# Softmax sums and reciprocals of two attention groups at a time, in a convolution layer with attention on one Trainium2 core

## The chip, the cores and the metric

The kernel runs on one core of one Trainium2 chip, in one launch, all data in 32-bit floats. The metric is device time in microseconds (us): the median of three runs before the change is 2254.44, from 2254.12 to 2254.50. Beside these runs one execution was recorded by the hardware profiler; durations of single instructions, waits and stretches come from that execution.

The engines are named as in the profile: PE is TensorE (PEld its weight loads), DVE is VectorE, ACT is ScalarE, POOL is GpSimd, and SP is SyncE, which issues most of the DMAs.

## The reference

The input is eight images of 512 channels, 32x32 pixels. The layer is `x + layer(groupnorm(x))`, where the layer is (cbs is a convolution, a batch norm with fixed statistics, and SiLU; C = 256, HEADS = 4, HD = 64, N = 2):

```python
def bot_attention(x, qkv_w, rw, rh):
    b, c, h, w = x.shape
    hw = h * w
    qkv = conv2d(x, qkv_w, 0).reshape(b, 3, HEADS, HD, hw)
    q, k, v = (qkv[:, 0], qkv[:, 1], qkv[:, 2])
    r = (rw + rh).reshape(1, HEADS, HD, hw)
    logits = jnp.einsum('bhdi,bhdj->bhij', q, k + r) * HD ** (-0.5)
    a = jax.nn.softmax(logits, axis=-1)
    out = jnp.einsum('bhij,bhdj->bhdi', a, v)
    return out.reshape(b, c, h, w)
t = cbs(x, cv1_w, cv1_bn, 0)
ys = [t[:, :C], t[:, C:]]
for i in range(N):
    yi = ys[-1]
    z = cbs(yi, m_cv1_w[i], m_cv1_bn[i], 1)
    z = bot_attention(z, m_qkv_w[i], m_rw[i], m_rh[i])
    z = jax.nn.silu(bn_eval(conv2d(z, m_cv2_w[i], 0), m_cv2_bn[i]))
    ys.append(yi + z)
return cbs(jnp.concatenate(ys, axis=1), cv2_w, cv2_bn, 0)
```

cv1, cv2 and m_cv2 are 1x1 convolutions, m_cv1 is a 3x3 one. The change concerns the softmax of the attention: the sum over the keys j for each query i, and the division by it.

## The kernel before

The eight images run as four pairs. In each pair every image passes cv1, and then twice the 3x3 convolution (over tiles of transformed inputs, L653 its matmuls), the projection to q, k and v (L886 to L1000), the attention and m_cv2 (m2, L1270). That makes 16 attentions. The long 1x1 products are built from sums of blocks, so that there are fewer matmuls. Work of other stages is threaded into an attention by hand: `behind` is a dictionary of hooks, keyed by the place in the attention, whose functions issue a step each of the next image's group norm (L718, L719, L725, L734 to L737), of the Winograd-like tile pieces (L559 to L608), of filters, or of the next product.

`attention_fast` works on four groups g = 0 to 3, each one chunk c of two heads and one half of the 1024 queries: (0,0), (0,1), (1,0), (1,1). A group has eight key blocks, taken in pairs, so that there are 16 pairs. Iteration i issues

- the logits of pair i (L1037, eight matmuls in the 64x64 form, which make 16 records of the profile), their exponentials on ScalarE (L1041), and the addition of the exponentials on VectorE into `acc` (L1055 for a group's first pair, which has no acc to add to, else L1057);
- then the product of pair i-1 with v (L1071), which adds up in `av_ps`.

At a group's end `av_ps` is copied out by ScalarE (L1078: one half) and VectorE (L1079: adds the other half to it, into z). `av_ps` comes from a PSUM pool with one buffer, so the next group's first L1071 waits for L1079 of this one. The pool of the logits has three buffers (tag "big"), which the sums (`s_ps`), m2 and the 1x1 products share. `acc` has two buffers in SBUF.

The sums over the partitions of a group's acc are made one group later, at the border: between the logits of the second pair of group g and the first product with v of group g, `sums(g - 1)` issues four matmuls of ones and acc (L1088, the 128x32 form, eight records). ScalarE copies the result to a row (L1094), and four DMAs on SP's queue and one reciprocal take it on its way: the row to DRAM (L1095), back in 128 partitions of eight numbers (`total`, L1124), the reciprocal (L1131), to DRAM again (L1133), and out to all partitions of a head (L1135, two DMAs of 128 KB for a group). The trip from L1124 on is issued in the third pair of group g (`spread`), and z is multiplied by it (`scale`, L1143) in the second pair of group g + 1.

The last group's sums, spread and scale are given to the caller, and stand in the next stage: group 2's scale follows directly on the last copy-out, and group 3's is issued after a part of the next product or projection. Then comes m2: for each half and each of two output chunks oc it adds k = 0 and k = 1. In the order of the code m2's eight matmuls need groups 0, 2, 0, 2 (first half) and 1, 3, 1, 3. The very first attention treats its last group by itself (`at_once`, L1105 and after).

The order on each engine comes from a scheduler that follows the order of the code, except where `issue_after` ties a step to another, and moves matmuls whose data are late behind others.

In the attentions 1, 5 and 9 the code threads tile pieces of the next convolution (from L555 on, each ends with a `yield`) at the keys (1, 3), (2, 1), (2, 3), 3 and (3, 2), where pairs and groups count from 0 and (g, n) stands after the products of pair n of group g with v; in attention 13 it does so at every (g, n) with n from 1 to 3. The piece at (1, 3) computes w_g (L566).

Of the kernel before, what the change touches and what calls it, by code (L numbers as in the profile page):

```python
# [44 lines left out]
F32 = mybir.dt.float32  # L45
# [7 lines left out]
P = 128  # L53
# [3 lines left out]
HD = 64  # L57
# [4 lines left out]
def kernel(  # L62
# [16 lines left out]
    nc = tc.nc  # L79
# [8 lines left out]
    HALF = 512  # L88
# [10 lines left out]
    NG = NM * NH  # L99
# [5 lines left out]
    act = fast.enter_context(tc.tile_pool(name="act", bufs=1))  # L105
# [167 lines left out]
    s_dram = [tc.dram_tile([P, KB, CO], F32, name=f"s{i}") for i in range(4)]  # L273
# [217 lines left out]
    def stages(act, small, ps_big, ps_av, n_pt):  # L491
# [522 lines left out]
        def attention_fast(qkv, ao, at, behind, at_once=False):  # L1014
# [35 lines left out]
            def add_up(pair):  # L1050
                g, j0 = pair[0]
                pt = pts[pair[0]]
                if j0 == 0:
                    accs[g] = act.tile([P, 2, HALF], F32, tag="acc", name="acc", bufs=2)
                    return nc.vector.tensor_tensor(accs[g], pt[0], pt[1], ALU.add)  # L1055
                for i in range(PAIR):
                    ins = nc.vector.tensor_tensor(accs[g], accs[g], pt[i], ALU.add)  # L1057
                return ins
# [19 lines left out]
                    nc.scalar.copy(dst, av[:, 0])  # L1078
                    evicted[0] = nc.vector.tensor_tensor(dst, av[:, 1], dst, ALU.add)  # L1079

            def sums(g):

                NQ4 = HALF // 2
                ps = ps_big.tile([P, NQ4], F32, tag="big", name="s_ps")
                acc = accs.pop(g)
                for at_q in range(4):
                    hd, part = divmod(at_q, 2)
                    nc.tensor.matmul(  # L1088
                        ps[at_q * 32 : (at_q + 1) * 32, :], ones[:, 0:32], acc[:, hd, ts(part, NQ4)],
                        start=True, stop=True, tile_position=(0, at_q * 32),  # L1090
                    )
                s_dram = tc.dram_tile([4, NQ4], F32, name=f"s_dram{at + g}")
                row = act.tile([P, NQ4], F32, tag="h", name="s_row", bufs=2)
                nc.scalar.copy(row, ps)  # L1094
                nc.sync.dma_start(s_dram, row[0:P:32, :])  # L1095
                return s_dram

            def last_sums(g):
# [20 lines left out]
                nc.sync.dma_start(cs, s_dram.rearrange("k h (i r) -> (h i) k r", r=QP))  # L1119
                nc.vector.tensor_tensor(sums_all[:, at + g, :], cs[:, 0], cs[:, 1], ALU.add)  # L1120

            def total(g, s_dram):

                nc.sync.dma_start(sums_all[:, at + g, :], s_dram.rearrange("a (i r) -> (a i) r", r=QP))  # L1124
                return sums_all[:, at + g, :]

            def spread(g, s_dram):

                rs = act.tile([P, HALF], F32, tag="rs", name="rs", bufs=4)
                rc = small.tile([P, QP], F32, tag="rc", name="rc", bufs=2)  # L1130
                inverted[0] = nc.vector.reciprocal(rc, total(g, s_dram))  # L1131
                r_dram = tc.dram_tile([2, HALF], F32, name=f"r_dram{at + g}")
                nc.sync.dma_start(r_dram.rearrange("h (i r) -> (h i) r", r=QP), rc)  # L1133
                for hd in range(2):
                    spread_out[0] = nc.sync.dma_start(  # L1135
                        rs[hd * HD : (hd + 1) * HD, :], r_dram[hd : hd + 1, :].to_broadcast([HD, HALF])
                    )
                return rs

            def scale(g, rs):  # L1140
                c, half = groups[g]
                dst = ao[:, c, ts(half, HALF)]
                return nc.vector.tensor_tensor(dst, dst, rs, ALU.mult)  # L1143

            NQ = NJ // PAIR
            s_drams, rss, evicted = {}, {}, [None]
            for i in range(len(pairs) + 1):
                if i < len(pairs):
                    added = logits(pairs[i])
                    g, at_q = divmod(i, NQ)  # L1150
                    with tc.issue_after(added.ins):
                        if at_q == NQ - 2 and g > 0:
                            rss[g - 1] = spread(g - 1, s_drams[g - 1])
                        if i == 1:
                            later()
                        if at_q == 1 and g > 1:
                            scale(g - 2, rss.pop(g - 2))
                if i > 0:
                    g, j0 = pairs[i - 1][0]
                    if j0 == 0 and g > 0:  # L1160
                        s_drams[g - 1] = sums(g - 1)
                    times_v(pairs[i - 1])
                    if i < len(pairs) and accs.get(pairs[i][0][0], 0) is None:
                        with tc.issue_after(evicted[0].ins):
                            added = add_up(pairs[i])
                    with tc.issue_after(added.ins):
                        behind.get(g if j0 == 0 else (g, j0 // PAIR), lambda: None)()
# [2 lines left out]

            g = len(groups) - 1
            if not at_once:
                with tc.issue_after(evicted[0].ins):
                    scale(g - 1, rss.pop(g - 1))
                return SimpleNamespace(
                    evicted=evicted[0], added=added,
                    sums=lambda: s_drams.update({g: sums(g)}),
                    spread=lambda: rss.update({g: spread(g, s_drams[g])}),
                    scale=lambda: scale(g, rss.pop(g)),
                )  # L1180
            ps, rows, s_dram = last_sums(g)
            with tc.issue_after(added.ins):
                behind.get(len(groups) + 1, lambda: None)()
            with tc.issue_after(evicted[0].ins):
                scale(g - 1, rss.pop(g - 1))
            rs = act.tile([P, HALF], F32, tag="rs", name="rs", bufs=4)
            nc.vector.tensor_tensor(rs, ps[:, 1, :], rows[0], ALU.add)
            nc.vector.reciprocal(rs, rs)
# [631 lines left out]
    for p in range(NP):  # L1820
# [117 lines left out]
        def hooks(norms, us={}, extra={}):  # L1938
            calls = {}
            for g in range(NG):  # L1940
                for at in range(4):
                    key = (g, at) if at else g
                    calls[key] = [step_norm] if key in norms else []
                    calls[key] += [step_u] * us.get(4 * g + at, 0)
                    if key in extra:
                        calls[key].append(extra[key])
            return {key: (lambda fs: lambda: [f() for f in fs])(fs) for key, fs in calls.items()}
# [126 lines left out]
            parts_at = (part for i in (1, 2) for part in tiles_later(i))  # L2074

        def step_part():
            next(parts_at, None)

        at_keys = ((1, 3), (2, 1), (2, 3), 3, (3, 2)) if more else [(g, at) if at else g for g in range(NG) for at in range(1, 4)]
        behind = hooks(NORM_B, {0: 1, 1: 1, 4: 1}, {key: step_part for key in at_keys})  # L2080
        if not more:
            tops = load_tops(ib, Y1[1])
            top_w = [take(("w2", j)) for j in range(2)]
            w2_top = lambda k: top_w[k // 2][:, k % 2]
            ys = {0: tops}

            def rhs_direct(k, half):
                part, c = divmod(k, NM)
                if part < 2:
                    return ys[0][half][part][:, c]  # L2090
                return ys[1][half][part - 2][:, c]
# [23 lines left out]
        def spread():  # L2115
            end.spread()
            return s.inverted[0]
# [246 lines left out]
```

## Time and profile before

| | us |
|---|---|
| median of three runs | 2254.44 |
| lowest, highest | 2254.12, 2254.50 |
| profiled execution: time | 2252.28 |
| profiled execution: span, first to last instruction | 2250.8 |
| TensorE busy in it | 2209.8 |
| VectorE, ScalarE, GpSimd busy | 1728.8, 1101.3, 225.1 |
| logits L1037 and products with v L1071, busy | 486.4, 485.9 |
| sums over partitions L1088: busy, records | 40.3, 504 |
| row copies L1094: busy, instructions | 23.9, 63 |
| reciprocals L1131: busy, instructions | 12.4, 63 |
| scales L1143: busy, instructions | 43.9, 64 |

The granted TensorE clock has a mean of 0.998 of full speed. Busy times count an instruction from its start to its end as the profile has it; records of TensorE overlap, so their sum is more than the time they cost. A line of groups names the line of the code, the engine, the operation, output and inputs by their names in the program, partitions by elements, how many there are, the busy time and the mean of one in ns, and after it the idle time of the engine before these instructions with what ended it. A line of the timeline has the start (us from the span's start), the time to the end of the last of its instructions, the engine, the line and the operation; in brackets, how long the engine stood idle before it and what ended that.

### The profile page before, as it was taken

What the parts mean: (1) busy time and instruction counts of PE and PEld (TensorE: products, weight loads), DVE (VectorE), ACT (ScalarE), POOL (GpSimd) and SP (SyncE); (2) the same over time, 40 slices, a digit from 0 to 9 for tenths busy, and PEclk for the clock granted to TensorE, in tenths of its full rate; (3) what the DMA queues carried; (4) which work ended last, traced back from release to release, by engine and by line L of the source; (5) the groups of instructions that cost most, each with busy time, mean ns of one, the idle gap of its engine ahead of it and who ended that gap; (6) DMA issues with size and microseconds to landing.
All of it is one profiled execution on the core that took longest, in us unless ns stands there. A gap on an engine that the chain in (4) does not pass through costs nothing.

```text
span 2250.8 us, 40563 instructions
## 1 busy us (share of the span) xinstructions
PE 2209.8 (98%) x16346; PEld 1079.1 (48%) x16346; DVE 1728.8 (77%) x2675; ACT 1101.3 (49%) x1359; POOL 225.1 (10%) x417
## 2 busy tenths in 40 slices
PE   7999999999999999999999999999999999999998
PEld 3653437343474445633447343654345733473443
DVE  7988879878678688877947868986794868796652
ACT  7554653644225765465324667355622455335533
POOL 4322210000220000000021000000012000000001
PEclk9999999999999999999999999999999999999999
DMA  9855447221581324521257151632136611351214
GB/s 276 309 157 150 155 148 260 91 93 50 135 269 59 113 88 143 178 64 65 66 154 260 30 173 35 198 111 82 51 79 176 226 44 34 102 192 35 67 46 111
DMA packets 135284, 285.63 MB, mean 127 GB/s; under 512 B 34512, under 2 KB 62156, under 8 KB 134064
## 3 DMA queue, kind: packets, MB, share of 16 engines
q1 hardware_dynamic: 103184, 197.34, 26.5%
q0 software_dynamic: 31904, 85.61, 13.2%
q8 instruction: 131, 2.15, 0.4%
q14 instruction: 65, 0.53, 0.1%
HBM read 214.86 MB, written 68.03 MB: 126 GB/s over the span
## 4 chain that ended last, share of the span: by engine, by line
PE 82%; DVE 11%; issue 3%; ACT 2%; DMA 1%; POOL 0%; SPq 0%; DVEq 0%; POOLq 0%; ACTq 0%
PE av_ps L1071 17%; PE l_ps L1037 16%; PE c L1290 9%; PE c_ps L653 7%; PE c_new L1290 6%; PE p_ps L916 6%; PE ps L523 5%; PE m_ps L1270 5%; PE x_ps L1390 4%; PE p_ps L922 3%; DVE acc L1057 1%; PE s_ps L1088 1%; PE p_ps L886 1%; DVE c_e L680 1%; ACT ypad L495 0%
## 5 line engine op out<-in xcount | busy, mean ns | idle before, releaser
L1041 ACT ACTIVATE pt<-l_ps 128x1024 f32<-128x1024 f32 x512 | 495.7, 1023 | 339.5 <-PE l_ps L1037 228.0
L1057 DVE TENSOR_TENSOR acc<-acc,pt 128x1024 f32<-128x1024 f32 x384 | 469.7, 1223 | 60.4 <-ACT pt L1041 34.9
L1037 PE MATMUL l_ps<-q,kr 64*64 64x512 f32 x4096 | 486.4, 590 | 2.4 <-ACT pt L1041 1.5
L1071 PE MATMUL av_ps<-pt,vT 64*64 64x512 f32 x4096 | 485.9, 591 | 1.8 <-DVE z L1079 1.5
L1037 PEld LDWEIGHTS l_ps<-q,kr 64*64 64x64 f32 x4096 | 158.0, 133 | 272.1 <-issue 251.0
L1071 PEld LDWEIGHTS av_ps<-pt,vT 64*64 64x64 f32 x4096 | 155.1, 133 | 275.3 <-issue 250.6
L653 PE MATMUL c_ps<-v_in,u 128*64 128x128 f32 x4320 | 239.1, 273 | 2.5 <-issue 2.5
L653 PEld LDWEIGHTS c_ps<-v_in,u 128*64 128x64 f32 x4320 | 235.8, 137 | 9.3 <-issue 9.3
L1270 PE MATMUL m_ps<-z,m_sb 128*128 128x512 f32 x256 | 112.5, 592 | 0.0
L658 ACT COPY c_m<-c_ps 128x512 f32<-128x512 f32 x48 | 28.1, 586 | 169.9 <-PE c_ps L653 153.1
L916 PE MATMUL p_ps<-t_z,sq 128*128 128x512 f32 x224 | 107.0, 595 | 0.0
L1079 DVE TENSOR_TENSOR z<-av_ps,z 128x512 f32<-128x512 f32 x64 | 44.0, 688 | 73.5 <-ACT z L1078 73.4
L495 ACT ACTIVATE t<-m_ps,bh,sh 128x512 f32<-128x512 f32 x64 | 46.3, 774 | 86.5 <-PE m_ps L1270 86.5
L916 PE MATMUL p_ps<-z,sq 128*128 128x512 f32 x168 | 80.1, 604 | 4.4 <-ACT z L495 4.3
L1055 DVE TENSOR_TENSOR acc<-pt 128x1024 f32<-128x1024 f32 x64 | 77.8, 1216 | 6.8 <-ACT pt L1041 6.8
L1340 POOL DMA_DIRECT2D c_out<-in_x_dram x56 | 50.3, 972 | 280.2 <-ACT c_out L495 276.8
L1270 PEld LDWEIGHTS m_ps<-z,m_sb 128*128 128x128 f32 x256 | 48.3, 190 | 58.8 <-issue 57.4
L1143 DVE TENSOR_TENSOR z<-z,rs 128x512 f32<-128x512 f32 x64 | 43.9, 686 | 26.0 <-DMA rs<-r_dram 25.9
L495 ACT ACTIVATE c_out<-cz,bh,sh 128x512 f32<-128x512 f32 x14 | 16.7, 1294 | 90.4 <-DVE cz L1367 90.4
L495 ACT ACTIVATE z<-z,bh,sh 128x512 f32<-128x512 f32 x64 | 47.7, 804 | 25.0 <-DVE z L704 24.3
L1390 PE MATMUL x_ps<-t_x,sw 128*128 128x512 f32 x128 | 55.9, 592 | 0.0
L922 PEld LDWEIGHTS p_ps<-sq,z 128*128 128x128 f32 x336 | 42.9, 191 | 26.3 <-issue 12.5
(313 smaller groups left out, 3153.7 us busy)
## 6 DMA issues: line engine op xcount, KB each, us to landing
u<-u SPq DMA_DIRECT2D x135, 512.0 KB
rs<-r_dram SPq DMA_DIRECT2D x126, 128.0 KB
sq<-sq SPq DMA_DIRECT2D x42, 384.0 KB
x<-in_x_dram SPq DMA_DIRECT2D x28, 512.0 KB
r_in<-r SPq DMA_DIRECT2D x28, 512.0 KB
y_in<-y SPq DMA_DIRECT2D x28, 512.0 KB
c_out<-in_x_dram POOLq DMA_DIRECT2D x56, 256.0 KB, 5.4
out_dram<-c_out POOLq DMA_DIRECT2D x56, 256.0 KB, 3.7
```

The costliest lines, as they stand in the source:

```text
L495: silued[0] = nc.scalar.activation(dst, src, AF.Silu, scale=sh[:, k : k + 1], bias=bh[:, k : k + 1])
L523: last_product[0] = nc.tensor.matmul(ps[:, half, :], w_of(k), rhs_of(k, half), start=(k == begin), stop=(k == end))
L653: conv_product[0] = nc.tensor.matmul(to[o], us[cp][:, k, row, c, o], rhs, start=(k == 0), stop=(k == NM - 1),)
L916: nc.tensor.matmul(ps[:, o, :], w[:, o, :], rhs, start=not onto, stop=True, skip_group_check=onto)
L922: nc.tensor.matmul(v[:, ts(j, P)], rhs[:, ts(j, P)], w[:, 2, :], start=j == 0 and not onto, stop=True, skip_group_check=True,)
L1037: nc.tensor.matmul(ps[kh * HD : (kh + 1) * HD, hd, :], kr[r, c, o : o + HD], q[r, c, ts(half, HALF)], start=True, stop=True,)
L1041: last_exp[0] = exp = nc.scalar.activation(pt, ps, AF.Exp, scale=SCALE)
L1057: ins = nc.vector.tensor_tensor(accs[g], accs[g], pt[i], ALU.add)
L1071: nc.tensor.matmul(avs[g][hd * HD : (hd + 1) * HD, kh, :], vT[r, j, o : o + HD], pt[i][r, hd, :], start=(j == 0), stop=(j == NJ - 1),)
L1270: nc.tensor.matmul(pss[half][:, oc, :], m2_sb[:, n, k, ts(oc, P)], ao[:, k, ts(half, HALF)], start=(k == 0), stop=(k == NM - 1),)
L1290: nc.tensor.matmul(ps[:, o, :], w[:, k, ts(o, P)], rhs[part][:, c], start=(k == 0 and not onto), stop=(k == KB - 1), skip_group_check=onto,)
L1390: nc.tensor.matmul(ps[:, o, :], w[:, c, ts(o, P)], rhs[c], start=(c == 0 and not onto), stop=(c == 1), skip_group_check=onto,)
```

## The change

The sums, the row copy, the DMA to DRAM and back, the reciprocal and the DMA of the reciprocals are made for two groups at a time, over one PSUM tile, one row and one DRAM tile: groups 0 and 1 at the border where group 2 begins, groups 2 and 3 after the end of the attention (attention 0, `at_once`: groups 0 and 1 together, group 2 by itself). The rs DMAs stay two for each group. The scales of groups 0 and 1 both stand in the second pair of group 3, and those of 2 and 3 both where group 3's stood. acc keeps its two buffers. A hook ("border", 2) is called at the border of group 2, between the copy-out and the group's first addition; in the attentions that carry tile pieces one piece moves there from the key (1, 3).

```diff
@@ -1078,21 +1078,22 @@
                     nc.scalar.copy(dst, av[:, 0])
                     evicted[0] = nc.vector.tensor_tensor(dst, av[:, 1], dst, ALU.add)
 
-            def sums(g):
+            def sums(gs):
 
                 NQ4 = HALF // 2
-                ps = ps_big.tile([P, NQ4], F32, tag="big", name="s_ps")
-                acc = accs.pop(g)
-                for at_q in range(4):
-                    hd, part = divmod(at_q, 2)
-                    nc.tensor.matmul(
-                        ps[at_q * 32 : (at_q + 1) * 32, :], ones[:, 0:32], acc[:, hd, ts(part, NQ4)],
-                        start=True, stop=True, tile_position=(0, at_q * 32),
-                    )
-                s_dram = tc.dram_tile([4, NQ4], F32, name=f"s_dram{at + g}")
-                row = act.tile([P, NQ4], F32, tag="h", name="s_row", bufs=2)
+                ps = ps_big.tile([P, len(gs), NQ4], F32, tag="big", name="s_ps")
+                for n, g in enumerate(gs):
+                    acc = accs.pop(g)
+                    for at_q in range(4):
+                        hd, part = divmod(at_q, 2)
+                        nc.tensor.matmul(
+                            ps[at_q * 32 : (at_q + 1) * 32, n, :], ones[:, 0:32], acc[:, hd, ts(part, NQ4)],
+                            start=True, stop=True, tile_position=(0, at_q * 32),
+                        )
+                s_dram = tc.dram_tile([len(gs), 4, NQ4], F32, name=f"s_dram{at + gs[0]}")
+                row = act.tile([P, len(gs), NQ4], F32, tag="h", name="s_row", bufs=2)
                 nc.scalar.copy(row, ps)
-                nc.sync.dma_start(s_dram, row[0:P:32, :])
+                nc.sync.dma_start(s_dram.rearrange("g a i -> a g i"), row[0:P:32])
                 return s_dram
 
             def last_sums(g):
@@ -1119,29 +1120,38 @@
                 nc.sync.dma_start(cs, s_dram.rearrange("k h (i r) -> (h i) k r", r=QP))
                 nc.vector.tensor_tensor(sums_all[:, at + g, :], cs[:, 0], cs[:, 1], ALU.add)
 
-            def total(g, s_dram):
-
-                nc.sync.dma_start(sums_all[:, at + g, :], s_dram.rearrange("a (i r) -> (a i) r", r=QP))
-                return sums_all[:, at + g, :]
-
-            def spread(g, s_dram):
-
-                rs = act.tile([P, HALF], F32, tag="rs", name="rs", bufs=4)
-                rc = small.tile([P, QP], F32, tag="rc", name="rc", bufs=2)
-                inverted[0] = nc.vector.reciprocal(rc, total(g, s_dram))
-                r_dram = tc.dram_tile([2, HALF], F32, name=f"r_dram{at + g}")
-                nc.sync.dma_start(r_dram.rearrange("h (i r) -> (h i) r", r=QP), rc)
-                for hd in range(2):
-                    spread_out[0] = nc.sync.dma_start(
-                        rs[hd * HD : (hd + 1) * HD, :], r_dram[hd : hd + 1, :].to_broadcast([HD, HALF])
-                    )
-                return rs
+            def total(gs, s_dram):
+                dst = sums_all[:, at + gs[0] : at + gs[0] + len(gs), :]
+                nc.sync.dma_start(dst, s_dram.rearrange("g a (i r) -> (a i) g r", r=QP))
+                return dst
+
+            def spread(gs, s_dram):
+
+                rc = small.tile([P, len(gs), QP], F32, tag="rc", name="rc", bufs=2)
+                inverted[0] = nc.vector.reciprocal(rc, total(gs, s_dram))
+                r_dram = tc.dram_tile([len(gs), 2, HALF], F32, name=f"r_dram{at + gs[0]}")
+                nc.sync.dma_start(r_dram.rearrange("g h (i r) -> (h i) g r", r=QP), rc)
+                rss = []
+                for n in range(len(gs)):
+                    rs = act.tile([P, HALF], F32, tag="rs", name="rs", bufs=4)
+                    for hd in range(2):
+                        spread_out[0] = nc.sync.dma_start(
+                            rs[hd * HD : (hd + 1) * HD, :], r_dram[n, hd : hd + 1, :].to_broadcast([HD, HALF])
+                        )
+                    rss.append(rs)
+                return rss
 
             def scale(g, rs):
                 c, half = groups[g]
                 dst = ao[:, c, ts(half, HALF)]
                 return nc.vector.tensor_tensor(dst, dst, rs, ALU.mult)
 
+            def scale_all(gs):
+                for g, rs in zip(gs, rss.pop(gs)):
+                    ins = scale(g, rs)
+                return ins
+
+            batch = {1: (0, 1), 2: (2,)} if at_once else {1: (0, 1), 3: (2, 3)}
             NQ = NJ // PAIR
             s_drams, rss, evicted = {}, {}, [None]
             for i in range(len(pairs) + 1):
@@ -1149,19 +1159,22 @@
                     added = logits(pairs[i])
                     g, at_q = divmod(i, NQ)
                     with tc.issue_after(added.ins):
-                        if at_q == NQ - 2 and g > 0:
-                            rss[g - 1] = spread(g - 1, s_drams[g - 1])
+                        if at_q == NQ - 2 and g - 1 in batch:
+                            gs = batch[g - 1]
+                            rss[gs] = spread(gs, s_drams[gs])
                         if i == 1:
                             later()
-                        if at_q == 1 and g > 1:
-                            scale(g - 2, rss.pop(g - 2))
+                        if at_q == 1 and g - 2 in batch:
+                            scale_all(batch[g - 2])
                 if i > 0:
                     g, j0 = pairs[i - 1][0]
-                    if j0 == 0 and g > 0:
-                        s_drams[g - 1] = sums(g - 1)
+                    if j0 == 0 and g - 1 in batch:
+                        s_drams[batch[g - 1]] = sums(batch[g - 1])
                     times_v(pairs[i - 1])
                     if i < len(pairs) and accs.get(pairs[i][0][0], 0) is None:
                         with tc.issue_after(evicted[0].ins):
+                            before = behind.get(("border", pairs[i][0][0]), lambda: None)() or evicted[0]
+                        with tc.issue_after(before.ins):
                             added = add_up(pairs[i])
                     with tc.issue_after(added.ins):
                         behind.get(g if j0 == 0 else (g, j0 // PAIR), lambda: None)()
@@ -1170,19 +1183,18 @@
 
             g = len(groups) - 1
             if not at_once:
-                with tc.issue_after(evicted[0].ins):
-                    scale(g - 1, rss.pop(g - 1))
+                gs = batch[g]
                 return SimpleNamespace(
                     evicted=evicted[0], added=added,
-                    sums=lambda: s_drams.update({g: sums(g)}),
-                    spread=lambda: rss.update({g: spread(g, s_drams[g])}),
-                    scale=lambda: scale(g, rss.pop(g)),
+                    sums=lambda: s_drams.update({gs: sums(gs)}),
+                    spread=lambda: rss.update({gs: spread(gs, s_drams[gs])}),
+                    scale=lambda: scale_all(gs),
                 )
             ps, rows, s_dram = last_sums(g)
             with tc.issue_after(added.ins):
                 behind.get(len(groups) + 1, lambda: None)()
             with tc.issue_after(evicted[0].ins):
-                scale(g - 1, rss.pop(g - 1))
+                scale_all(batch[g - 1])
             rs = act.tile([P, HALF], F32, tag="rs", name="rs", bufs=4)
             nc.vector.tensor_tensor(rs, ps[:, 1, :], rows[0], ALU.add)
             nc.vector.reciprocal(rs, rs)
@@ -2074,10 +2086,11 @@
             parts_at = (part for i in (1, 2) for part in tiles_later(i))
 
         def step_part():
-            next(parts_at, None)
-
-        at_keys = ((1, 3), (2, 1), (2, 3), 3, (3, 2)) if more else [(g, at) if at else g for g in range(NG) for at in range(1, 4)]
+            return next(parts_at, None)
+
+        at_keys = ((2, 1), (2, 3), 3, (3, 2)) if more else [(g, at) for g in range(NG) for at in range(1, 4) if (g, at) != (1, 3)]
         behind = hooks(NORM_B, {0: 1, 1: 1, 4: 1}, {key: step_part for key in at_keys})
+        behind["border", 2] = step_part
         if not more:
             tops = load_tops(ib, Y1[1])
             top_w = [take(("w2", j)) for j in range(2)]
```

## The prediction, on record before the run

> Attentions are counted 0 to 15 in the order they run, groups 0 to 3 inside each; a border is where one group ends and the next begins. Line numbers are those of the kernel before.
>
> **What bounds the kernel now.** I read the page first: which engine is full, and what the chain that ended last consists of.
>
> ```profile
> span 2250.8 us, 40563 instructions
> ...
> PE 2209.8 (98%) x16346; PEld 1079.1 (48%) x16346; DVE 1728.8 (77%) x2675; ACT 1101.3 (49%) x1359; POOL 225.1 (10%) x417
> ...
> PE 82%; DVE 11%; issue 3%; ACT 2%; DMA 1%; POOL 0%; SPq 0%; DVEq 0%; POOLq 0%; ACTq 0%
> ```
>
> TensorE is the bound, and only 41 us of the span are left in which it does nothing. So the change pays only in TensorE time, and whatever it delays elsewhere costs as soon as TensorE waits for it. Next the groups that the change touches:
>
> ```profile
> L1079 DVE TENSOR_TENSOR z<-av_ps,z 128x512 f32<-128x512 f32 x64 | 44.0, 688 | 73.5 <-ACT z L1078 73.4
> L1143 DVE TENSOR_TENSOR z<-z,rs 128x512 f32<-128x512 f32 x64 | 43.9, 686 | 26.0 <-DMA rs<-r_dram 25.9
> ...
> L1088 PE MATMUL s_ps<-acc,ones 128*32 128x256 f32 x504 | 40.3, 391 | 2.2 <-DVE gm L734 1.4 <-DVE acc L1057 0.6
> ```
>
> 504 records are 63 stretches of 8 (attention 0 has three, its last group goes another way). What one stretch costs is not 8 x 391 ns, since records overlap; it is read from the starts, in the timeline round an ordinary border:
>
> ```profile
> 703.62 1.90 PE L1037 MATMUL l_ps<-q,kr 64*64 64x512 f32 x16
> ...
> 705.34 1.90 PE L1071 MATMUL av_ps<-pt,vT 64*64 64x512 f32 x16
> ...
> 707.05 1.90 PE L1037 MATMUL l_ps<-q,kr 64*64 64x512 f32 x16
> ...
> 707.92 0.69 DVE L1079 TENSOR_TENSOR z<-av_ps,z 128x512 f32<-128x512 f32 x1
> ...
> 708.53 1.22 DVE L1055 TENSOR_TENSOR acc<-pt 128x1024 f32<-128x1024 f32 x1
> ...
> 708.88 0.64 PE L1088 MATMUL s_ps<-acc,ones 128*32 128x256 f32 x8
> ...
> 709.45 1.95 PE L1071 MATMUL av_ps<-pt,vT 64*64 64x512 f32 x16
> ...
> 711.22 1.90 PE L1037 MATMUL l_ps<-q,kr 64*64 64x512 f32 x16
> ```
>
> Without sums, logits follow values after 1.715 us (703.62, 705.34, 707.05). Across the border the same two steps take 711.22 - 707.05 = 4.17 instead of 3.43: one stretch costs 0.74. The second four of its records begin 0.215 after the first four, so streaming is 2 x 0.215 = 0.43; the other 0.31 goes into entering and leaving the 128x32 form.
>
> **The Trainium skill.** "TensorEngine Tiling (Array Packing)", section "Key Properties", says that a change of tiling mode drains TensorE; the 0.31 agrees in sign, the page has no price. "DMA: Bandwidth & Descriptors", "Anatomy of one DMA", gives some 2.0 us of fixed cost a DMA, mostly the write receipt, with descriptor generation "small, variable". That is for transfers issued from GpSimd; here, issued from SP, the sums' read lands 1.7 us and r_dram 1.4 us after issue in the quick cases, so two small transfers in one should cost little more than one. No row shows a transfer of 256 descriptors. "Perfetto Trace Analysis", "Optimizing Scalar/DVE Operations", has a fixed access cost for each VectorE instruction: the reciprocal of 8 columns takes 197 ns, and 16 will hardly take more.
>
> **The change, part by part.**
>
> *Fewer stretches.* 63 become 32 (two in each attention). 31 x 0.74 = 22.9 us go; their 31 x 0.43 = 13.3 us of streaming come back in the stretches that stay. Gain 31 x 0.31 = 9.6 us. Bounds: nothing, if the 0.31 belongs to each eight records (a rival below), and 12, if streaming shares its drain. In attention 2 a scale that waited 3.64 us for rs delayed the copy-out at a border; that scale goes, TensorE's 0.59 of waiting with it: 10.2.
>
> *Fewer row copies, reciprocals and small DMAs* (31 of each, x 380 and x 197 ns, and 3 x 31 issues on SP): ScalarE, VectorE and SP are covered by TensorE there, since in the 980 us of attention TensorE is busy 974 and VectorE 830. Nothing, either way. The 126 rs transfers stay.
>
> *The cover of the copy-out goes.* The values of a new group need the one av slot, free when L1079 ends. In the timeline it ends at 708.61, 0.15 before the logits do: enough without the stretch. I went through the removed borders for those where it ends later. In attentions 5, 9 and 13 at the first border (statistics L718/L719 or a tile piece L579 stand ahead of it on VectorE) it ends 0.87 to 0.90 after; attention 3 0.56 after. The stretch covered 0.57. Without it TensorE waits: 3 x 0.69 + 0.62 = 2.7 us. Bounds 2 to 3.5.
>
> *A new wait.* acc has two buffers, and group 2's first add (L1055) now takes the one that holds group 0's sums, read only in that same border. It waits for the stretch's first half: 0.64 + 0.06 after its start, some 1.0 us of VectorE. Queued behind it are the adds L1057 of the group, and through them exp buffers. Group 2 has one scale (0.69) less, and the next copy-out has 1 to 3 us of slack in most (0.26 in attentions 6 and 10): nothing. In attentions 1, 5, 9 and 13 a w_g piece (1.2 us) fills the wait. But in attentions 4 and 8 a group norm of the next image stands there:
>
> ```profile
> 722.99 1.22 DVE L1055 TENSOR_TENSOR acc<-pt 128x1024 f32<-128x1024 f32 x1
> 724.12 0.15 DVE L734 COPY gm<-gm_ps 128x4 f32<-128x4 f32 x1
> ...
> 724.33 0.64 PE L1088 MATMUL s_ps<-acc,ones 128*32 128x256 f32 x8 [0.72 <-DVE gm L734]
> ...
> 724.90 0.21 PEld L1071 LDWEIGHTS av_ps<-pt,vT 64*64 64x64 f32 x8 [0.41 <-ACT pt L1041]
> ```
>
> gm's copy stands behind the first add. In the changed order the stretch can start at 723.61, the add at 724.31, the copy at 725.44, the values (which need its slot) at about 725.65, 0.32 later than counted; L735 to L737 lie between further adds until 728.5, where TensorE, ready at 727.6, waits about 1.0 for gv_ps. 1.2 to 1.3 each: 2.4 us. Bounds 1 to 3.5.
>
> *The attention's end.* m2 (L1270, eight matmuls of 0.86) has in its second one group 2's values. Their scale stood right after the last copy-out; now it comes with group 3's, after a trip of the sums to DRAM and back. In the built order m2 therefore begins with its first and fifth matmul, then other work, then the second. In ends followed by a projection (2, 6, 10, 12, 14) the second comes 0.86 + 0.86 + 0.22 = 1.94 us after m2's start, and the last scale ended at +1.73, held by VectorE's queue and not by rs; in ends followed by a convolution (3, 7, 11, 15) it comes at +2.58, and the scale ended at +2.03 to +2.35. With two scales the first takes that place. I estimate the trip's growth at 1.1: row copy 380 to about 590 ns (its 256 columns doubled), and 0.45 for each of the two transfers with twice the rows; the first half of it is hidden in most, as the reciprocal waited for VectorE. I take 0.2 in all; bounds 0 and 9. Attentions 5 and 9:
>
> ```profile
> 869.63 7.03 PE L1270 MATMUL m_ps<-z,m_sb 128*128 128x512 f32 x16
> 869.83 2.29 ACT L495 ACTIVATE y_half<-x_ps,bh,sh 128x512 f32<-128x512 f32 x2 [1.42 <-PE x_ps L1390]
> ...
> 871.03 0.69 DVE L1143 TENSOR_TENSOR z<-z,rs 128x512 f32<-128x512 f32 x1 [1.26 <-DMA rs<-r_dram]
> ...
> 878.90 1.22 DVE L559 SCALAR_TENSOR_TENSOR w_ba<-ypad 128x1024 f32<-128x1024 f32 x1
> ```
>
> The filler is two x_ps matmuls (1.72), which need the slot that L495 frees at 872.12; TensorE is there at 871.35 + release: 0.83 of waiting each, 1.7. They also push m2's results back. VectorE is busy without a gap from 878.87 to 910.46, and there TensorE already waits for it:
>
> ```profile
> 910.56 2.70 PE L653 MATMUL c_ps<-v_in,u 128*64 128x128 f32 x45 [0.63 <-issue]
> ```
>
> Some 1.75 us (the filler's own length) pass through: 3.5 for both; bounds 0 (if VectorE's pieces before 878 leave room) and 3.5.
>
> *Sum.* Gains 10.2. Losses 2.7 + 2.4 + 0.2 + 1.7 + 3.5 = 10.5. Net +0.3. The profiled execution, 2252.28 (its span and 1.5 around it), would be 2252.6; the median of the three runs is 2.16 above the profiled one, so 2254.44 + 0.3 = 2254.7. A measurement of this kernel tells about 0.2%, 4.5 us, from no change.
>
> **The rivals.**
> A, the forecast: gain and losses cancel; 2250 to 2258.5 by the middle of the bounds.
> B, the covers hold: the gm wait, the x_ps filler and the convolution's VectorE find slack elsewhere, and only the late copy-outs cost: 10.2 - 2.7 = 7.5 gained, 2247. For it: TensorE waits in few places now, and a stall can use up a later wait. Against it: VectorE shows no gap where I put the losses.
> C, slower: the trip is too long for m2's second matmul. It decides from a growth of about 1.2 us on; each further 0.1 costs 0.1 in nine ends, 0.9. With 1 us more 9 us, 2264; with 0.5 more, 2259. For it: an end's slack is 0.1 to 0.3, and the doubled descriptors are unseen. Against it: the skill's fixed cost, and rs issues that now wait up to 3.5 us behind others on SP.
> D, it doesn't do what it says: the 0.31 comes with each eight records and is not saved. Then the 9.6 are gone, and 9.9 lost: 2264. Against it: nothing changes form inside a joined stretch.
>
> **How the numbers follow.** A 0.42, B 0.37, C 0.16, D 0.05. The range runs from 2245 (B with a gain at its upper bound) to 2262 (the milder half of C). Faster by over 0.2% (below 2249.9): nearly all of B and A's edge, 0.36; slower (above 2258.9): C and D with A's edge, 0.21; within: 0.43.
>
> **What would show it.** Right: 32 stretches of 16 records, each some 1.17 us between logits and values beyond the step; waits of 0.6 to 0.7 for L1079 at the first border of 5, 9 and 13; waits for gm and gv in 4 and 8; a wait in the x_ps filler of 5 and 9, and a longer one before the convolution that follows. Wrong: a joined stretch of 1.5 (D), waits of m2 for the scale in most ends (C), or none of the listed waits (B).

## The result and the profile after

| | before | changed |
|---|---|---|
| median of 13 runs, us | 2254.27 | 2259.09 |
| lowest, highest | 2252.47, 2255.65 | 2257.39, 2260.93 |
| profiled execution: span | 2250.8 | 2256.5 |

The changed kernel is 4.8 us slower: ratio 1.0021, 95% interval 1.0012 to 1.0029. The forecast was +0.3. The range of 2245 to 2262 holds the measured time; the side it fell on, slower than 2258.9, was given 0.21.

The lines of the page and of the groups that answer to those shown of before:

```profile
span 2256.5 us, 40228 instructions
...
PE 2203.3 (98%) x16346; PEld 1082.8 (48%) x16346; DVE 1731.0 (77%) x2644; ACT 1100.0 (49%) x1328; POOL 223.1 (10%) x417
...
PE 76%; DVE 18%; issue 2%; ACT 1%; POOL 0%; DVEq 0%; ACTq 0%
```

```profile
L1055 DVE TENSOR_TENSOR acc<-pt 128x1024 f32<-128x1024 f32 x64 | 78.0, 1218 | 20.4 <-PE s_ps L1089 13.6 <-ACT pt L1041 6.8
L1079 DVE TENSOR_TENSOR z<-av_ps,z 128x512 f32<-128x512 f32 x64 | 44.0, 687 | 76.2 <-ACT z L1078 76.1
L1147 DVE TENSOR_TENSOR z<-z,rs 128x512 f32<-128x512 f32 x64 | 42.6, 686 | 29.7 <-DMA rs<-r_dram 29.5
L1089 PE MATMUL s_ps<-acc,ones 128*32 128x256 f32 x504 | 33.8, 385 | 0.5 <-ACT pt L1041 0.5
```

TensorE is busy 6.5 us less and the span is 5.7 longer: 12.2 us more in which TensorE does nothing. VectorE has gone from 11% to 18% of the chain that ended last, and the first add now waits 13.6 us for the sums, which it never did. What TensorE waits for is the next view (columns: total us, times, longest), first of before, then of the changed kernel:

```profile
PE p_ps L916 <- ACT z L495: 4.3, 5, 0.9
...
PE c_ps L653 <- issue: 2.5, 4, 0.6
...
PE av_ps L1071 <- DVE z L1079: 1.5, 5, 0.5
...
PE gv_ps L725 <- DVE dev L737: 0.9, 1, 0.9
```

```profile
PE p_ps L916 <- ACT z L495: 6.1, 7, 0.9
PE c_ps L653 <- issue: 5.6, 6, 1.7
...
PE gv_ps L725 <- DVE dev L737: 3.6, 4, 1.2
PE av_ps L1071 <- DVE z L1079: 2.8, 4, 1.0
...
PE x_ps L1402 <- ACT y_half L495: 1.2, 2, 0.6
```

These waits understate the loss, since the profile models the ends of matmuls; their starts are recorded. So I cut both executions at the first L1037 and last L1071 of each attention and at the first and last m2 record, and took the differences of the stretches. An ordinary attention with its end (6, 10, 12, 14) is 1.03 shorter inside and 0.43 longer behind: 0.60 gained, where the forecast had 0.62. In the table, the first row takes this 0.60 for each of 15 attentions, with 0.30 for attention 0 and 0.66 for attention 2's wait; the other rows are what the stages differ from it:

| term | forecast | profiles |
|---|---|---|
| fewer stretches, attention 2's wait with them | -10.2 | -10.0 |
| late copy-outs, attentions 3, 5, 9, 13 | +2.7 | +3.0 |
| attentions 4 and 8 (group norm) | +2.4 | +4.5 |
| ends of 5 and 9: filler and convolution | +5.2 | +5.1 |
| ends of 3, 7, 11, 15 and the stage after | +0.2 | +2.3 |
| attentions 1, 7, 11, small waits | 0 | +0.9 |
| sum | +0.3 | +5.8 |

The sum ends at TensorE's last matmul; what follows that was 0.3 shorter, so the span is 5.65 longer. What lies ahead of attention 0 is left out: it is the same program in every kernel here, and was up to 2.2 us longer in some profiled executions, which is why medians and not spans give the verdicts.

An ordinary joined border, and an end that a projection follows, in the changed kernel's timeline:

```profile
976.54 1.90 PE L1037 MATMUL l_ps<-q,kr 64*64 64x512 f32 x16
...
978.37 1.07 PE L1089 MATMUL s_ps<-acc,ones 128*32 128x256 f32 x16
979.08 1.23 DVE L1055 TENSOR_TENSOR acc<-pt 128x1024 f32<-128x1024 f32 x1 [0.97 <-PE s_ps L1089]
979.37 1.95 PE L1071 MATMUL av_ps<-pt,vT 64*64 64x512 f32 x16
...
981.14 1.90 PE L1037 MATMUL l_ps<-q,kr 64*64 64x512 f32 x16
```

```profile
1017.91 1.88 PE L1282 MATMUL m_ps<-z,m_sb 128*128 128x512 f32 x4
1018.96 0.68 DVE L1147 TENSOR_TENSOR z<-z,rs 128x512 f32<-128x512 f32 x1
1019.63 0.39 PE L922 MATMUL p_ps<-sq,t_z 128*128 128x128 f32 x2
1019.85 0.59 PE L1282 MATMUL m_ps<-z,m_sb 128*128 128x512 f32 x1
```

Two steps across the border take 4.60 instead of 3.43: 1.17, the forecast's number. The first add waits 0.97, and TensorE doesn't notice. In the end, m2's second product comes at +1.94, and the scale it needs ended at +1.73: no wait.

### The profile page after: what moved, and what is told of

It is laid out like the page before. It is cut to its first block, busy times and chain, and to the rows that moved or that the text cites. A ratio compares the mean times of both kernels' runs of the same rounds, so it can differ in the third digit from the quotient of the medians.

```text
span 2256.5 us, 40228 instructions
## 1 busy us (share of the span) xinstructions
PE 2203.3 (98%) x16346; PEld 1082.8 (48%) x16346; DVE 1731.0 (77%) x2644; ACT 1100.0 (49%) x1328; POOL 223.1 (10%) x417
## 4 chain that ended last, share of the span: by engine, by line
PE 76%; DVE 18%; issue 2%; ACT 1%; POOL 0%; DVEq 0%; ACTq 0%
PE av_ps L1071 17%; PE l_ps L1037 16%; PE c L1302 9%; PE c_new L1302 6%; PE p_ps L916 6%; PE ps L523 5%; PE m_ps L1282 5%; PE c_ps L653 4%; PE x_ps L1402 3%; DVE acc L1057 3%; PE p_ps L922 3%; PE s_ps L1089 1%; DVE c_e L680 1%; DVE c_t L673 1%; DVE c_t L672 1%
## 5 line engine op out<-in xcount | busy, mean ns | idle before, releaser
L1037 PE MATMUL l_ps<-q,kr 64*64 64x512 f32 x4096 | 491.4, 590 | 3.0 <-ACT pt L1041 1.9
L1071 PE MATMUL av_ps<-pt,vT 64*64 64x512 f32 x4096 | 489.6, 590 | 3.2 <-DVE z L1079 2.8
L1071 PEld LDWEIGHTS av_ps<-pt,vT 64*64 64x64 f32 x4096 | 158.7, 133 | 284.3 <-issue 231.3
L1037 PEld LDWEIGHTS l_ps<-q,kr 64*64 64x64 f32 x4096 | 160.4, 133 | 272.0 <-issue 244.7
L1055 DVE TENSOR_TENSOR acc<-pt 128x1024 f32<-128x1024 f32 x64 | 78.0, 1218 | 20.4 <-PE s_ps L1089 13.6
```

What stands on the lines that cost most here:

```text
L1037: nc.tensor.matmul(ps[kh * HD : (kh + 1) * HD, hd, :], kr[r, c, o : o + HD], q[r, c, ts(half, HALF)], start=True, stop=True,)
L1071: nc.tensor.matmul(avs[g][hd * HD : (hd + 1) * HD, kh, :], vT[r, j, o : o + HD], pt[i][r, hd, :], start=(j == 0), stop=(j == NJ - 1),)
```

## The experiments

My theory after the result: the saving of 0.31 a stretch is real; it is eaten where a separate stretch had covered something on VectorE or ScalarE, and where work was put into m2. Rivals: nothing is saved by joining; or all of the loss is the joined trip at the end. Each kernel is compared with the kernel before on the same chip; the changed kernel's own difference is +4.8, between +2.7 and +6.5 by its interval. The edits are shown shortened.

**The price of a stretch.** Four more matmuls in every stretch of the kernel before:

```diff
-    for at_q in range(4):
-        nc.tensor.matmul(ps[at_q * 32 : (at_q + 1) * 32, :], ...)
+    for n in range(2):
+        for at_q in range(4):
+            nc.tensor.matmul(ps[at_q * 32 : (at_q + 1) * 32, n, :], ...)
```

> The kernel before with every stretch of sums made twice over in the same stretch (the second copy is used): 63 stretches of 16 records in place of 8, all else as before. My theory (0.43 us to stream, 0.31 to enter and leave): 63 x 0.43 = +27 us, about 2281. Rival 'the 0.31 comes with every eight records': 63 x 0.74 = +47, about 2301.

Measured: 2279.57 against 2254.62, +25.0 (ratio 1.0109, 1.0093 to 1.0124). 25.0 / 63 = 0.40 for eight more records, at most 0.44 by the interval; 0.74 is excluded. Joining saves what it was meant to save.

**One half of the change each.** `batch` is all that differs, beside the scale of group 2 and the key of the tile piece:

```diff
-batch = {1: (0, 1), 2: (2,)} if at_once else {1: (0, 1), 3: (2, 3)}
+batch = {1: (0, 1), 2: (2,)} if at_once else {1: (0, 1), 2: (2,), 3: (3,)}
```
```diff
-batch = {1: (0, 1), 2: (2,)} if at_once else {1: (0, 1), 3: (2, 3)}
+batch = {0: (0,), 1: (1,), 2: (2,)} if at_once else {0: (0,), 1: (1,), 3: (2, 3)}
```

> Only groups 0 and 1 are summed together; groups 2 and 3 keep their own sums, trips and scales as before. My theory (a stretch less saves 0.31 us, and waits that the joining brings eat it): the joined border alone loses, above all in attentions 4 and 8, where TensorE waits for gv_ps, and at late copy-outs; from the stages of the changed kernel's trace, +3.7 us against before, about 2258.0. Rival 'the end is all of it' (the loss comes only from the joined trip at the attention's end): 16 x 0.31 = 5 us gained, about 2249.3. Rival 'nothing is saved by joining': +8, about 2262.

> Only groups 2 and 3 are summed together, the tile piece is back at its old key, groups 0 and 1 are as before. My theory: 15 stretches less and the wait for rs in attention 2 gain 11.7 - 6.5 = 5.2, the ends lose 7.5: +2.3 against before, about 2256.5. Rival 'the end is all of it': the loss of the changed kernel and the 5 us that pairing 0 and 1 gains: +10, about 2264. Rival 'nothing is saved by joining': +7, about 2261.

Measured: 0 and 1 together 2255.60 against 2254.62, ratio 1.0005 (0.9996 to 1.0013): between -0.9 and +2.9, so the 5 us of gain are excluded and the +3.7 is missed. 2 and 3 together 2257.67, ratio 1.0013 (1.0006 to 1.0019): +3.0, where +2.3 was expected. By the medians neither half has the whole loss.

**Attentions 4 and 8.** The changed kernel at the border of group 2:

```profile
720.91 0.22 PE L725 MATMUL gm_ps<-mv,gmat 64*64 64x4 f32 x2 [0.53 <-DVE mv L719]
...
723.23 1.07 PE L1089 MATMUL s_ps<-acc,ones 128*32 128x256 f32 x16 [0.27 <-ACT pt L1041]
723.93 1.23 DVE L1055 TENSOR_TENSOR acc<-pt 128x1024 f32<-128x1024 f32 x1 [2.18 <-PE s_ps L1089]
724.23 2.79 PE L1071 MATMUL av_ps<-pt,vT 64*64 64x512 f32 x18
...
725.08 0.15 DVE L734 COPY gm<-gm_ps 128x4 f32<-128x4 f32 x1
...
727.92 0.16 DVE L737 TENSOR_TENSOR dev<-dev,mv 128x4 f32<-128x4 f32 x1
728.23 0.22 PE L725 MATMUL gv_ps<-dev,gmat 64*64 64x4 f32 x2 [1.22 <-DVE dev L737]
```

The values start at 724.23, ahead of gm's copy; 18 records take 1.93 at the usual pace (16 in 1.715), so TensorE had work until about 726.16 and lost 2.07 before gv_ps. Two experiments: the norm's steps one key earlier, and these two attentions unpaired.

```diff
-NORM_A = ((0, 2), (0, 3), (1, 1), (1, 2), (1, 3), 2, (2, 1), (2, 2), (2, 3), 3)
+NORM_A = ((0, 1), (0, 2), (0, 3), (1, 1), (1, 2), (1, 3), 2, (2, 1), (2, 2), (2, 3))
```

> The changed kernel with the group norm's steps one key earlier in the attentions that carry them at the first image (0,1) to (2,3) in place of (0,2) to 3, so that gm is read and dev is made before the add that waits. My theory: the 2 us of gv_ps and the 0.5 us of gm_ps in each of attentions 4 and 8 go: 4 to 5 us less than the changed kernel, about 2254.5. Rival 'the gv wait is hidden by a later wait anyway' (or the end is all of it): no change, about 2259.

Measured: 2257.85 against 2254.62, +3.2, 1.6 less than the changed kernel: my expectation of 4 to 5 fell. By the stages only 0.3 came back in each of the two attentions. The wait for gv is gone, but the same attention now waits at its other two borders, where there is no stretch any more:

```profile
710.87 0.66 PE L1071 MATMUL av_ps<-pt,vT 64*64 64x512 f32 x4 [0.79 <-DVE z L1079]
...
739.56 1.27 ACT L809 ACTIVATE x<-x,shift,gr 128x1024 f32<-128x1024 f32 x1
740.69 0.61 ACT L1078 COPY z<-av_ps 128x512 f32<-128x512 f32 x1
741.34 0.69 DVE L1079 TENSOR_TENSOR z<-av_ps,z 128x512 f32<-128x512 f32 x1 [2.92 <-ACT z L1078]
...
742.08 0.66 PE L1071 MATMUL av_ps<-pt,vT 64*64 64x512 f32 x4 [1.19 <-DVE z L1079]
```

Statistics moved ahead of the first copy-out, and the normalization (L809) ahead of the third. Unpairing instead:

```diff
+if n_att[0] in (4, 8):
+    batch = {0: (0,), 1: (1,), 3: (2, 3)}
```

> The changed kernel with groups 0 and 1 kept apart in attentions 4 and 8 alone. My theory: the changed kernel's +1.2 us in each of these two attentions becomes -0.0, as with groups 2 and 3 paired alone: 2.4 us less, about 2256.7. Rival (what the run with the group norm's steps moved suggested, that another step only takes over the wait): 0.5 us less, about 2258.5.

Measured: 2257.41 against 2254.55, +2.9: 2.0 less than the changed kernel. The intervals of the two kernels overlap (this one's is 1.0006 to 1.0020), so it is the profile that decides: each of the two attentions goes from +1.2 to -0.01, as the theory said.

**Attentions 5 and 9.** The changed kernel at the end of 5, and in the convolution after it:

```profile
870.80 1.88 PE L1282 MATMUL m_ps<-z,m_sb 128*128 128x512 f32 x4
...
872.28 0.69 DVE L1147 TENSOR_TENSOR z<-z,rs 128x512 f32<-128x512 f32 x1 [1.21 <-DMA rs<-r_dram]
...
873.30 1.98 PE L1402 MATMUL x_ps<-t_x,sw 128*128 128x512 f32 x4 [0.61 <-ACT y_half L495]
...
875.12 5.31 PE L1282 MATMUL m_ps<-z,m_sb 128*128 128x512 f32 x12
```

```profile
903.00 10.70 PE L653 MATMUL c_ps<-v_in,u 128*64 128x128 f32 x192 [1.66 <-issue]
```

The scale ends at 872.97 and the second product starts at 875.12, so the trip isn't what it waits for: the filler is. Both of its costs are there, its own wait and the convolution's (2.2 in two waits, where before had 0.63). Two kernels, the first with groups 2 and 3 apart in these two attentions, the second with m2's loops turned round in every attention:

```diff
+elif n_att[0] not in (5, 9):
+    batch[3] = (2, 3)
+else:
+    batch.update({2: (2,), 3: (3,)})
```
```diff
-for half in range(NH):
-    for oc in range(NM):
-        for k in range(NM):
+for k in range(NM):
+    for half in range(NH):
+        for oc in range(NM):
```

> The changed kernel with groups 2 and 3 kept apart in attentions 5 and 9 alone. My theory: 2 x 2.3 us come back, about 2254.5. Rival 'the waits of the convolution there have another cause': under 1 us, about 2258.5.

> The changed kernel, with m2 adding all four k = 0 products (groups 0 and 1) before the four k = 1 products (groups 2 and 3), so that m2 has 3.4 us of its own work before it needs group 2's scale and no other matmul is put into it. My theory: the 2.6 us that each of the ends of attentions 5 and 9 lost come from the two x_ps matmuls put into m2, and go at least for the most part: 3 to 5 us less than the changed kernel, about 2255. Rival 'the later trip and scale are what delays VectorE there, whatever stands in m2': no gain, about 2259.

Measured: apart, 2255.45 against 2254.55, +0.9, 3.9 less than the changed kernel; m2's order, 2254.55 against 2254.55 (0.9990 to 1.0007), 4.8 less. With k = 0 first, m2 is one piece, and the scales are there in time although they wait for rs no less (2.25 in all after 5, 1.84 in the changed kernel):

```profile
871.59 7.03 PE L1282 MATMUL m_ps<-z,m_sb 128*128 128x512 f32 x16
872.66 0.69 DVE L1147 TENSOR_TENSOR z<-z,rs 128x512 f32<-128x512 f32 x1 [1.02 <-DMA rs<-r_dram]
874.58 0.69 DVE L1147 TENSOR_TENSOR z<-z,rs 128x512 f32<-128x512 f32 x1 [1.23 <-DMA rs<-r_dram]
```

By the stages 3.2 of the gain lie at 5 and 9. There m2 itself costs nothing more, but the convolution after it is still 0.6 and 1.3 longer than before: its waits are 1.1 and 1.7, where the changed kernel had 2.2 and the kernel before 0.63. With groups 2 and 3 apart they are 0.6. So the filler is not all of the convolution's loss; a part stays as long as groups 2 and 3 are joined there. Why that part was 0.6 at one place and 1.3 at the other is open.

**The trip alone.** Stretches and row copies as before, one row tile for two groups, and everything after it joined:

```diff
+nc.scalar.copy(row_of[gs][:, g - gs[0], :], ps)   # at each group's own border
 nc.sync.dma_start(s_dram.rearrange("g a i -> a g i"), row[0:P:32])
```

> The trip alone: each group keeps its own stretch of sums at its own border and its own row copy, as before, but row, transfers, reciprocal and scales are joined for two groups as in the changed kernel; the tile piece is back at its old key. My theory: no stretch is saved and no copy-out loses its cover, the ends lose what they lose in the changed kernel (2 x 2.6 in attentions 5 and 9, and what a late scale costs elsewhere), 5 to 7 us more than before, about 2260. Rival 'the joined trip is harmless, the loss comes from joining the matmuls': as before, about 2254.5.

Measured: 2258.28 against 2254.79, +3.5 (1.0010 to 1.0026, so +2.3 to +5.9): the middle is below the 5 to 7 expected, and the rival, no loss, falls. The profiled execution, the longest of the fourteen (2260.23), is 6.6 longer beyond the start-up: the ends of 5 and 9 lose 2.60 each again, while attentions 4 and 8 gain 0.55 each and attention 2 gains 0.66, which I had not counted. What sets that execution apart from the median is open.

**The stages after 3, 7 and 11.** The table's +2.3 was in no case of mine. VectorE does the same operations in the same order there, but one of them takes longer; first the kernel before ahead of attention 4, then the changed kernel:

```profile
665.23 0.69 DVE L693 TENSOR_TENSOR c_k<-c_r 128x512 f32<-128x512 f32 x1
...
666.28 0.56 POOL L1341 DMA_DIRECT2D out_dram<-c_out  x1 [1.69 <-DMA c_out<-in_x_dram]
...
666.86 1.28 POOL L900 TENSOR_TENSOR t_z<-z 128x512 f32<-128x512 f32 x1
...
667.64 0.80 DVE L689 TENSOR_TENSOR c_r<-c_t 128x256 f32<-128x256 f32 x1
```

```profile
663.29 0.56 POOL L1353 DMA_DIRECT2D out_dram<-c_out  x1 [2.21 <-PE c_ps L653]
...
663.87 1.29 POOL L900 TENSOR_TENSOR t_z<-z 128x512 f32<-128x512 f32 x1
663.88 1.84 DVE L693 TENSOR_TENSOR c_k<-c_r 128x512 f32<-128x512 f32 x1
665.64 0.68 DVE L694 TENSOR_TENSOR c_k<-c_r 128x512 f32<-128x512 f32 x1
...
677.55 0.70 PE L916 MATMUL p_ps<-z,sq 128*128 128x512 f32 x1 [0.87 <-ACT z L495]
```

L693 takes 0.69 alone, and 1.84 beside the subtraction L900 on GpSimd. The Trainium skill, "SBUF — State Buffer", section "SBUF: two separate sides", describes a port pair that VectorE and GpSimd lock for a whole instruction, VectorE also for operations with two inputs in SBUF, against a GpSimd operation that reads SBUF. The traces agree: L693 ends 0.56 after L900, and operations that read PSUM (L672, L673, L680) keep their 0.68 beside it. The page gives the pair to the one that starts first; that the starts here don't show, for two of the long operations (2.14 and 1.98) began 0.30 and 0.13 ahead of L900 and ended 0.56 after it. What L900 hits depends on its moment: ahead of 4, 8 and 12 it starts as soon as GpSimd has issued an output DMA (L1341, in the changed kernel L1353). Ahead of attention 4 it comes 3.0 earlier than before, while VectorE is only 1.4 earlier. Before, a long hit (1.87) fell ahead of attention 8 alone, 0.4 of delay ahead of 4 and 12; in the changed kernel there are 1.84, 2.14 and 1.98 ahead of 4, 8 and 12. The edit takes L900 off GpSimd:

```diff
-t = first_sum(summed, nc.gpsimd)
+t = first_sum(summed)
```

> The changed kernel with the subtraction L900, which GpSimd does near the end of a convolution, on VectorE. My theory (a VectorE operation between tensors in SBUF that begins beside L900 is held until that ends, and what it hits is chance): the operations of 1.65 to 2.14 us on VectorE become 0.4 to 0.7, L900's own 0.7 comes on, and TensorE's wait of 0.87 for z ahead of attentions 4, 8 and 12 falls to about 0.4: 1 to 2 us less than the changed kernel, about 2257.8. Rival 'VectorE is late there because of the moved scale and its wait for rs': no gain, 2259 or more.

Measured: 2255.22 against 2254.79, +0.4: 4.4 less than the changed kernel, twice what I expected. In the profile the stretches ahead of 4, 8 and 12 are 0.8 to 1.0 shorter, and those ahead of 6, 10 and 14 0.2 to 0.5, which I had not counted. Of these 4.0 us some 2.1 are what the change had added ahead of 4 and 12. The rest isn't: the stage ahead of 8 is now 0.8 shorter than in the kernel before, that ahead of 14 0.2, so the edit also takes away a cost that was there already. The kernel before with this edit alone was not run. The timeline at the same place:

```profile
664.52 0.69 DVE L900 TENSOR_TENSOR t_z<-z 128x512 f32<-128x512 f32 x1
665.12 0.69 DVE L693 TENSOR_TENSOR c_k<-c_r 128x512 f32<-128x512 f32 x1
...
677.66 1.12 PE L916 MATMUL p_ps<-z,sq 128*128 128x512 f32 x2 [0.15 <-ACT z L495]
```

**What is left when the losses are avoided.** First the selection (below), then with m2's order and groups 2 and 3 together in 3, 7, 11 and 13 too, then with L900 on VectorE as well:

```diff
+if n_att[0] in (0, 2, 6, 7, 10, 11, 12, 14, 15):
+    batch = {1: (0, 1)}
+else:
+    batch = {0: (0,), 1: (1,)}
...
+elif n_att[0] in (1, 2, 6, 10, 12, 14, 15):
+    batch[3] = (2, 3)
```

> Groups 0 and 1 are summed together only in attentions 0, 2, 6, 7, 10, 11, 12, 14, 15, groups 2 and 3 only in 1, 2, 6, 10, 12, 14, 15: where the two half changes lost nothing. My theory: the gain of the stretches alone is left, 8 x 0.30 + 0.96 and some 2.0 from the ends: 5.4 us less than before, about 2249. Rivals 'nothing is saved by joining' and 'the savings are used up by waits that follow anyway': as before, about 2254.5.

> The selection of the earlier run (groups 0 and 1 together in attentions 0, 2, 6, 7, 10, 11, 12, 14, 15) with m2's four k = 0 products first, and so with groups 2 and 3 together in four more attentions: 1, 2, 3, 6, 7, 10 to 15. My theory: with m2's own work ahead of the second scale the four ends lose nothing and gain some 0.2 each: 0.7 us less than the selection alone, about 2248.6. Rival 'm2's outputs all come late with that order and the convolution after it waits': 1 to 2 us more than the selection, about 2251.

> The selection with m2's k = 0 products first, and L900 on VectorE as well. My theory: the two gains add up, since they lie in different stretches: 2248.5 less the 3.9 that L900 gave on the changed kernel, about 2244.6. Rival 'L900 on VectorE only helped since the changed kernel had made VectorE late': 2248 or more.

Measured: selection 2249.34 against 2254.55, -5.2 (ratio 0.9974, 0.9965 to 0.9984); with m2's order 2248.50 against 2254.79, -6.3 (0.9972, 0.9962 to 0.9983), which the intervals don't tell from the selection; with L900 on VectorE 2244.50 against 2253.87, -9.4 (0.9958, 0.9944 to 0.9971), the best here. The rivals of these three runs fall. The selection's gain is that of joining alone. Of the -9.4 some 3 are L900's; whether they can be had without any joining was not run.

## Why the prediction was right and wrong

- *The gain*: right, -10.0 of -10.2, by the 0.31 a stretch that an ordinary attention shows. Rival D fell. One reading was off: the second four records of a stretch begin 0.24 after the first four, not 0.215; only in a joined stretch the third and fourth four follow by 0.216. So 0.43 for eight more is right.
- *Late copy-outs*: right, 3.0 of 2.7, at the attentions named (waits of 0.73, 0.73 and 1.00 in 5, 9 and 13, and 0.33 in 3).
- *Ends of 5 and 9*: right in place and size, 5.1 of 5.2: 0.88 each in m2 beyond the filler's own length, 1.69 each in the convolution. The mechanism is right in part: without the filler its wait goes, but 0.6 and 1.3 of the convolution's loss stay. Only keeping the groups apart took both.
- *m2's second product in other ends* (rival C): no wait, as taken; the ends that a convolution follows lost otherwise. The trip grew by less than the 1.1 estimated: from the row copy to the reciprocal it took 4.19 in place of 3.77 (medians of 15 ends), where the estimate had 0.66 for this part.
- *Attentions 4 and 8*: right in place, half in size. The step that failed is "the values (which need its slot) at about 725.65": they start at 724.23, ahead of the copy, so TensorE comes to gv_ps at about 726.16, not 727.6, and loses 2.07 there, not 1.0. The wait of 0.53 for gm_ps was not in the sum: TensorE, with a stretch of 0.74 less behind it, comes there before the statistics are ready.
- *The stages after 3 and 11*: missing from the sum. I took VectorE's durations there as fixed; 1.84 for a 0.69 operation stands beside a GpSimd operation, and the moment of that one, after an output DMA, decides which operation is hit. The long operation was in the trace of before too (1.87).
- *The forecast* of +0.3 was thus 4.5 low by the medians and 5.5 by the profiles: 2.1 in attentions 4 and 8, 2.1 in the convolution stages, 0.9 in small waits, 0.3 in copy-outs. It called no change beyond 0.2% the likeliest; 4.8 us are just beyond that, and 2259.09 just above the 2258.5 that ended A's own bounds. That it lies inside the range is partly luck: the range reaches to 2262 for rival C, whose mechanism no end showed. Rival B, that the covers hold, was given 0.37 and fell in all its parts.

Open: where 2.2 us of the kernel that joins groups 0 and 1 alone went, whose profile has +3.2 without the start-up and whose median has +1.0. The profiles of the other kernels, too, stand 0.2 to 1.8 above their medians, and that of the trip alone 3.1: all are set against one profiled execution of before, and the moment at which L900 falls may differ from execution to execution, which one profile can't show.

## What to carry to other kernels

A short stretch on the busy engine can be the cover of another engine's work at the same place; before joining stretches, list what ended just in time under each that goes. Joining is worth a change-over each (0.31 us here), so do it only where nothing was hidden: here 16 places of 31 gained 5 us, while all 31 together cost 5. When a late operand moves into a product, give the product its own early terms first, rather than let other work be put in.

## What the runs showed of the hardware

Entering and leaving the 128x32 form between 64x64 matmuls cost 0.31 us here (0.74 for a stretch less 0.43 for its records), and eight more records in the form 0.40 by the medians, 0.43 in the trace. VectorE operations on two SBUF inputs that met L900 on GpSimd (1.28 us) ended 0.28 to 0.56 after it and took 0.77 to 2.14 instead of 0.41 to 0.69. In the changed kernel ahead of 6 and 10, where such operations of 0.41 were under way as L900 began, they kept their 0.41 and L900 took 2.03; the next one took 1.65. Joining two trips cost little in instructions: the row copy went from 380 to 589 ns with twice the columns, the reciprocal from 197 to 248.
